# Two folded cross attentions in a twelve-block network: query folding in pieces among the steps, normalisation in two halves, the output projection in two parts, the last batch in halves

## The chip, the cores and the metric

The kernel runs on one core of one Trainium2 chip. It is one program that computes a whole Perceiver-like network of twelve blocks in float32. The metric is the device time of one execution in microseconds (us), taken from the first to the last instruction, as a median over runs. The engines are TensorE (PE in the profile, with PEld for its weight loads), VectorE (DVE), ScalarE (ACT), GpSimd (POOL) and SyncE (SP, here a DMA queue).

## The reference

Twelve blocks follow each other, each with a residual connection. The change touches the two blocks marked below; they are the same computation with different weights, on a batch of 16, with 64 queries of width 256 and a context of 1024 keys of width 192 for each element.

```python
def _layernorm(x, axis=-1, eps=1e-05):
    m = jnp.mean(x, axis=axis, keepdims=True)
    v = jnp.var(x, axis=axis, keepdims=True)
    return (x - m) / jnp.sqrt(v + eps)

def _L1_xattn_ref(x, context, Wq, Wk, Wv, Wo, bo):      # _L2_xattn_ref computes the same
    h, d = (8, 64)
    scale = d ** (-0.5)
    q = (x @ Wq).reshape(B, Sq, h, d).transpose(0, 2, 1, 3)
    k = (context @ Wk).reshape(B, -1, h, d).transpose(0, 2, 1, 3)
    v = (context @ Wv).reshape(B, -1, h, d).transpose(0, 2, 1, 3)
    scores = jnp.einsum('bhid,bhjd->bhij', q, k) * scale
    attn = jax.nn.softmax(scores, axis=-1)
    out = jnp.einsum('bhij,bhjd->bhid', attn, v)
    out = out.transpose(0, 2, 1, 3).reshape(B, Sq, h * d)
    return out @ Wo + bo

x = x + _L0_xattn_ref(...)   # then _L0_attn_ref, _L0_ffn_ref
x = x + _L1_xattn_ref(_layernorm(x, axis=-1), ctx_768, ...)   # touched by the change
...                          # _L1_attn_ref, _L1_ffn_ref
x = x + _L2_xattn_ref(_layernorm(x, axis=-1), ctx_768, ...)   # touched by the change
...                          # _L2_attn_ref, _L2_ffn_ref, and the three blocks of L3
```

## The kernel before

The 1024 tokens (16 batch elements of 64 queries) lie in `X` as eight tiles of 128 tokens; `xn` is the normalised form and `xnT` its transpose. `xattn_folded` computes both touched blocks, called with `"L1_xattn"` and `"L2_xattn"`; below they are the second and the third cross attention. Keys are never projected: the query is multiplied by the key weights instead ("folded"), so that scores are `qw` times the raw context.

- **Prologue.** `norm_T` (lines 244 to 262) normalises and transposes all eight tiles, in two halves of four tiles. After it every instruction of TensorE, VectorE and ScalarE is put into a fixed order by `set_order(True)`: each engine's instructions are chained in the order of the Python text (`in_order`, line 172). What is issued through plain `nc.…` calls, POOL work and DMAs, is placed by the framework's scheduler.
- **Folding.** `queries(g, m)` projects two heads (index `m`, four of them) for a group `g` of four batch elements into a bank `psq`, which ScalarE scales into `qT`. `fold(g, m)` multiplies by the key weights into two banks `psqw`, one copied into `qw` by VectorE, one by ScalarE. `folded(g)` does all four `m` in a row: once in the prologue, and then in front of the first scores of every next group, three times. `qw` has one buffer for a whole group.
- **Steps.** There are 32 steps, one for each batch element `b` and half `h` of the eight heads. In step `i` TensorE computes the scores of the step ahead (four banks `pss`; first the 128 rows of context, then `sums` of the present step into `psm`, then the other 64 rows), and then the `values` of the batch element before (four of eight key chunks a step), and in odd steps its `others` (the remaining 64 context channels). VectorE takes the reciprocal of the sums, the row minimum of the negated scores (`least`: tiles `nm`, `nw`, `nmm`), half of the `shares` (normalising the probabilities), and two 32-by-32 transposes (`turn`, tile `pT`). ScalarE does the other half of the shares, the eight `exps` (tile `pr`), and copies.
- **Output.** `keep` copies the finished sums into `oc`. After every four batch elements, in the even step of the next but one, `output(g2)` projects by the value weights (`pso`, copied to `oT`) and by the output weights (`psy`), and adds into `X`.
- **PSUM banks.** `ps_s` has five banks in turn (tag `s`: `pss`, `psq`, `psqw`, one `pso`); `ps_t` has one (tag `t`: `psm`, one `pso`, `psy`); `ps_o` has two (`o0`, `o1`).
- **Extra work in the steps.** In the second cross attention `conv_taps` (POOL, ScalarE and VectorE, tile `tapp`) runs in steps 3 to 11 for the block after. In the third `ctx_sigma` runs on VectorE in every odd step (eight pairs of statistics, then a root on POOL). `add_row` adds the output's bias to all eight tiles of `X` on POOL (eight instructions, line 157); it is ordered behind the last root.

The order inside a step is the order of this text:

```python
prs, sm = now
if ahead:
    pss = scores(*ahead, lambda: sums(st, sm))
dve.reciprocal(sm, st["sum"][:, :8])
shares(prs, sm, 1)
if ahead:
    now = exps(pss, least(pss))
shares(prs, sm, 0)
turn(b, 2 * h, prs[0])
```

Of the kernel before, what the change touches and what calls it, by code (L numbers as in the profile page):

```python
# [15 lines left out]
P = 128  # L16
# [62 lines left out]
class Net:  # L79
# [428 lines left out]
    def xattn_folded(self, L):  # L508
# [18 lines left out]
        with ExitStack() as es:  # L527
# [9 lines left out]
            self.norm_T(ps_s, "s")  # L537
            self.set_order(True)
            qws, qTs, ctxs, cxs, pTs, outs, ocs = ({} for _ in range(7))

            def bank(name):
                return ps_s.tile([P, 512], F32, tag="s", name=name)

            def queries(g, m):
# [3 lines left out]
                ps = bank("psq")  # L548
# [4 lines left out]
            def fold(g, m):  # L553


                if m == 0:
                    qws[g] = two.tile([P, 2, G, H, TQ], F32, tag="qw", name="qw", bufs=1)
                qT = qTs[m]
                pss = [bank("psqw") for _ in range(2)]
# [4 lines left out]
                for hh, copy in enumerate((dve.tensor_copy, act.copy)):  # L564
                    copy(qws[g][:, :, :, 2 * m + hh, :], pss[hh].rearrange("p (i b q) -> p i b q", i=2, q=TQ))

            def folded(g):
                queries(g, 0)
                for m in range(4):
                    if m < 3:  # L570
                        queries(g, m + 1)
                    fold(g, m)
# [17 lines left out]
            def scores(b, h, between):  # L590
# [4 lines left out]
                qw = qws[b // G]  # L595
                pss = [bank("pss") for _ in range(4)]

                def score(k, u, i, rows, start, stop):
                    for qa in range(4):
                        self.mm(  # L600
                            pss[k][qa * 32 : (qa + 1) * 32, u * 256 : (u + 1) * 256],
                            qw[rows, i, b % G, 4 * h + k, u * 32 : (u + 1) * 32],
# [66 lines left out]
            def values(b, r):  # L669

                if r == 0:
                    outs[b] = [ps_o.tile([P, 512], F32, tag=n, name=n) for n in ("o0", "o1")]
                for j in range(4 * r, 4 * r + 4):
                    self.mm(outs[b][0], cxs[b][:, j, 0:P], pTs[b][:, j], j == 0, j == NKC - 1)

            def others(b):

                for j in range(NKC):
                    rows = slice((j % 2) * 64, (j % 2 + 1) * 64)
                    self.mm(outs[b][1][rows, :], cxs[b][:, j, P:C], pTs[b][:, j], j < 2, j >= NKC - 2)  # L680
# [8 lines left out]
            def output(g2):  # L689
                oc = ocs[g2]  # L690
                oT = one.tile([P, 4, T2], F32, tag="oT", name="oT")
# [14 lines left out]
                for tt in range(T2 // P):  # L706
                    t = g2 * T2 // P + tt
                    ps = ps_t.tile([P, 512], F32, tag="t", name="psy")
                    for m in range(4):
                        self.mm(ps[:, :D], oT[:, m, tt * P : (tt + 1) * P], wo[:, m, :], m == 0, m == 3)  # L710
# [44 lines left out]
            for r in range(2):  # L755
                values(B - 1, r)
# [1921 lines left out]
```

## Time and profile before

| what | value |
|---|---|
| runs | 3168.56, 3169.97 and 3195.57 us; median 3169.97 us |
| profiled execution | 3170.8 us, of which the span of its instructions is 3168.8 us |
| TensorE busy | 2940.9 us, 93% of the span |
| VectorE, ScalarE, GpSimd busy | 1960.3, 1348.4, 712.7 us |
| mean granted TensorE clock | 0.953 |
| second cross attention, first scores to last `psy` matmul | 766.8 to 1207.5 us |
| third cross attention, first scores to last `psy` matmul | 1659.2 to 2098.6 us |

A busy TensorE is not one that works at its peak: the ends of matmuls are modelled, and a matmul at half the granted clock counts as busy for twice as long. The stage tables give the granted clock beside the busy times. In a timeline, a bracket behind an instruction says how long its engine had stood idle and what released it.

### The profile page before, as it was taken

How to read it: one execution, taken by the hardware profiler on the slowest of the kernel's cores; microseconds unless marked ns; L12 is line 12 of the kernel's file. 1: busy time of each engine (PE TensorE's matmuls, PEld its weight loads, DVE VectorE, ACT ScalarE, POOL GpSimd, SP SyncE). 2: the span in 40 equal slices, each digit the busy share in tenths (PEclk: the TensorE clock that was granted, in tenths of full speed). 3: DMA queues.
4: the chain of work that ended last, by engine and by line, in shares of the span. 5: the costliest groups of instructions: out<-in, count | busy, mean ns of one | idle time of the engine just before them, and what ended most of it. 6: DMA issues, size and time to landing. Idle time of an engine off the chain costs nothing.

```text
span 3168.8 us, 64106 instructions
## 1 busy us (share of the span) xinstructions
PE 2940.9 (93%) x26912; PEld 1772.9 (56%) x26912; DVE 1960.3 (62%) x4061; ACT 1348.4 (43%) x3035; POOL 712.7 (22%) x784
## 2 busy tenths in 40 slices
PE   7999999898899999979978999997999899998797
PEld 4666666665445544458854545434665455556676
DVE  6888886524666665971127676757884676765611
ACT  3555554312554541013324454438861255654211
POOL 1000002411110001014411000024771355541131
PEclk9999999999999999978988999998999999999889
DMA  2000000013223313017851222201111211210233
GB/s 74 32 32 32 28 22 15 14 37 105 61 78 92 98 45 82 21 65 270 294 162 53 70 71 73 59 21 39 41 54 37 64 57 63 70 44 14 94 108 122
DMA packets 73793, 223.00 MB, mean 70 GB/s; under 512 B 17457, under 2 KB 28580, under 8 KB 66594
## 3 DMA queue, kind: packets, MB, share of 16 engines
q1 hardware_dynamic: 45936, 113.99, 11.9%
q0 software_dynamic: 21840, 99.39, 9.4%
q10 hardware_dynamic: 5730, 5.53, 0.6%
q8 instruction: 212, 3.47, 0.5%
q14 instruction: 75, 0.61, 0.1%
HBM read 210.00 MB, written 12.66 MB: 70 GB/s over the span
## 4 chain that ended last, share of the span: by engine, by line
PE 79%; DVE 9%; issue 4%; ACT 4%; POOL 3%; DMA 1%; SPq 0%; ACTq 0%; POOLq 0%; DVEq 0%
PE pss L188 13%; PE o L188 12%; PE pu L188 6%; PE psp L188 5%; PE pkv L188 5%; PE pd L188 5%; PE py L188 4%; PE pst L191 4%; PE psc L188 3%; PE po L188 2%; DVE nm L72 2%; ACT pr L72 2%; PE pb L191 2%; PE psi L188 1%; PE psq L188 1%
## 5 line engine op out<-in xcount | busy, mean ns | idle before, releaser
L188 PE MATMUL pss<-cT,qw 128*32 128x256 f32 x8192 | 371.5, 387 | 23.0 <-ACT pr L72 23.0
L72 DVE TENSOR_REDUCE nm<-pss 128x2 f32<-128x512 f32 (+1 forms) x384 | 309.3, 861 | 86.3 <-PE pss L188 86.3
L188 PE MATMUL o<-pT,cx 128*64 128x512 f32 (+1 forms) x1024 | 355.4, 607 | 0.0
L72 ACT ACTIVATE pr<-pss,nmm 128x256 f32<-128x256 f32 x512 | 234.3, 483 | 164.8 <-DVE nmm L72 164.8
L188 PEld LDWEIGHTS pss<-cT,qw 128*32 128x32 f32 x8192 | 205.0, 110 | 173.0 <-ACT pr L72 33.1
L188 PEld LDWEIGHTS o<-pT,cx 128*64 128x64 f32 (+1 forms) x1024 | 127.8, 165 | 200.2 <-issue 187.8
L205 POOL TENSOR_SCALAR rs<-mv 128x8 f32<-128x8 f32 (+3 forms) x52 | 10.0, 193 | 877.1 <-DVE mv L221 444.4
L188 PE MATMUL pkv<-wx,cT 128*128 128x512 f32 (+1 forms) x512 | 193.3, 632 | 0.6 <-issue 0.6
L72 ACT ACTIVATE pr<-pr,sm 128x256 f32<-128x256 f32 x256 | 109.1, 497 | 184.2 <-DVE sm L72 184.2
L72 DVE TENSOR_SCALAR pr<-pr,sm 128x256 f32<-128x256 f32 (+1 forms) x384 | 170.6, 486 | 6.6
L72 DVE TENSOR_TENSOR_SCAN h<-dA,pb 128x512 f32<-128x512 f32 x128 | 154.5, 1217 | 15.8 <-PE pb L191 9.4
L1444 POOL TENSOR_TENSOR h<-h,cb 128x1024 f32<-128x1024 f32 x64 | 151.4, 2368 | 53.3 <-DVE h L72 51.0
L2304 DVE TENSOR_SCALAR y<-pd,row 128x256 f32<-128x256 f32 x39 | 18.9, 484 | 225.1 <-PE pd L188 175.7
L72 DVE STREAM_TRANSPOSE pT<-pr 128x1024 f32<-128x1024 f32 x128 | 151.8, 1224 | 2.2
L188 PE MATMUL pd<-wd,hT 128*128 128x256 f32 x656 | 149.3, 382 | 3.0 <-DVE hT L2492 1.4
L72 ACT ACTIVATE pr<-pss,nm 128x1024 f32<-128x1024 f32 x128 | 142.5, 1113 | 11.4 <-DVE nm L72 8.8
L191 PE MATMUL pst<-ident,pr 128*128 128x128 f32 x1024 | 140.6, 280 | 5.8 <-DVE sm L72 1.9
L72 ACT COPY pT<-pst 128x512 f32<-128x512 f32 x128 | 74.9, 585 | 163.8 <-PE pst L191 163.8
L191 PEld LDWEIGHTS pst<-ident,pr 128*128 128x128 f32 x1024 | 109.4, 141 | 61.5 <-ACT pT L72 26.5
L188 PEld LDWEIGHTS pd<-wd,hT 128*128 128x128 f32 x656 | 123.1, 190 | 31.4 <-DVE hT L2492 6.2
L1618 POOL TENSOR_TENSOR rnk<-rnk,mhalf 128x8 f32<-128x8 f32 (+1 forms) x84 | 130.0, 1548 | 7.0
L188 PE MATMUL py<-h,ident 128*128 128x512 f32 x256 | 130.7, 596 | 0.0
(525 smaller groups left out, 5700.2 us busy)
## 6 DMA issues: line engine op xcount, KB each, us to landing
cT<-in_ctxT SPq DMA_DIRECT2D x32, 768.0 KB, 4.4
cx<-in_ctxP SPq DMA_DIRECT2D x32, 768.0 KB, 4.3
cT<-in_ctxT SPq DMA_DIRECT2D x32, 512.0 KB, 4.3
cT<-in_ctxT SPq DMA_DIRECT2D x64, 256.0 KB, 6.1
offb<-d_off SPq DMA_DIRECT2D x16, 576.0 KB, 3.6
cb<-d_C SPq DMA_DIRECT2D x16, 512.0 KB, 3.8
wu<-in_L_ffn_w POOLq DMA_DIRECT2D x8, 1024.0 KB
wd<-in_L_ffn_w POOLq DMA_DIRECT2D x8, 1024.0 KB
```

What stands on the lines that cost most here:

```text
L72: ins = getattr(self.engine, op)(*args, **kwargs)
L188: self.in_order(self.nc.tensor.matmul(out, lhsT=lhsT, rhs=rhs, start=start, stop=stop))
L191: self.in_order(self.nc.tensor.transpose(out, in_, self.ident))
L205: nc.gpsimd.tensor_scalar(t[:p, :n], in_, scale, eps, ALU.mult, ALU.add)
L1444: nc.gpsimd.tensor_tensor(hs[i], hs[i], cbs[hf, g], ALU.mult)
L1618: nc.gpsimd.tensor_tensor(r, r, self.mhalf[:, : n * H], ALU.pow)
L2304: nc.vector.tensor_scalar(y[:, i, :], po[:, i * D : (i + 1) * D], weight[:, g + i : g + i + 1], None, ALU.mult)
```

## The change

`norm_T` in the prologue gives way to `norm(g)` and `normed(g)` for four tiles each: `norm(0)` and `normed(0)` stay in the prologue, `norm(1)` comes at the end of step 1 and `normed(1)` at the end of step 2. `folded` is gone. `queries` and `fold` are called for one piece (two heads of a group) at a time: pieces 0 and 1 of group 0 ahead of the first scores, pieces 2 and 3 behind the first `exps`; the pieces of group 1 in steps 0, 1, 6 and 7, of group 2 in steps 10, 12, 14 and 15, of group 3 in steps 18, 20, 22 and 23. `qw` becomes three buffers of half a group's heads. `psq` and one of the two `psqw` move from the five banks to the single bank of `ps_t`. `output` is cut into `heads` (in the even step, as before) and `output(t)` for two tiles at the end of the odd step behind it. In the last step the `values` of the element before go ahead of the `sums`, and the last batch element's `values` and `others` are computed for 256 of 512 columns at a time. `add_row` moves from step 2 to step 5.

```diff
-            self.norm_T(ps_s, "s")
...
+            def norm(g):
+                ts = slice(4 * g, 4 * g + 4)
+                for t in range(4 * g, 4 * g + 4):
+                    dve.bn_stats(stats[:, t, :], self.X[:, t, :])
+                    dve.bn_aggr(mv[:, t, :], stats[:, t, :])
+                self.rsqrt(rs[:, ts], mv[:, ts, 1], 1.0, 1e-5, 4)
+            def normed(g):
+                for t in range(4 * g, 4 * g + 4):
+                    dve.tensor_scalar(
+                        self.xn[:, t, :], self.X[:, t, :], mv[:, t, 0:1], rs[:, t : t + 1], ALU.subtract, ALU.mult
+                    )
+                for c, copy in enumerate((dve.tensor_copy, act.copy)):
+                    ps = bank("psT")
+                    for k in range(4):
+                        self.tr(ps[:, k * P : (k + 1) * P], self.xn[:, 4 * g + k, c * P : (c + 1) * P])
+                    copy(self.xnT[:, c, g * 512 : (g + 1) * 512], ps)
 
             def queries(g, m):
-                ps = bank("psq")
+                ps = ps_t.tile([P, 512], F32, tag="t", name="psq")
...
             def fold(g, m):
-                if m == 0:
-                    qws[g] = two.tile([P, 2, G, H, TQ], F32, tag="qw", name="qw", bufs=1)
+                if m % 2 == 0:
+                    qws[g, m // 2] = two.tile([P, 2, G, 4, TQ], F32, tag="qw", name="qw", bufs=3)
                 qT = qTs[m]
-                pss = [bank("psqw") for _ in range(2)]
+                pss = [bank("psqw"), ps_t.tile([P, 512], F32, tag="t", name="psqw")]
...
-            def values(b, r):
+            def values(b, js, cols=slice(0, 512)):
...
-            def output(g2):
+            def heads(g2):
...
+            def output(t):
+                ps = ps_t.tile([P, 512], F32, tag="t", name="psy")
...
-            folded(0)
+            norm(0)
+            normed(0)
+            for m in range(2):
+                queries(0, m)
+                fold(0, m)
             steps = [(b, h) for b in range(B) for h in range(2)]
             pss = scores(0, 0, None)
             now = exps(pss, least(pss))
+            for m in range(2, 4):
+                queries(0, m)
+                fold(0, m)
+            pieces = {8 * g + at: (g + 1, m) for g in range(B // G - 1) for m, at in enumerate((2, 4, 6, 7))}
+            pieces.update({0: (1, 0), 1: (1, 1)})
+            del pieces[2], pieces[4]
             for i, (b, h) in enumerate(steps):
                 ahead = steps[i + 1] if i + 1 < len(steps) else None
-                if ahead and ahead[0] % G == 0 and ahead[1] == 0:
-                    folded(ahead[0] // G)
+                piece = pieces.get(i)
...
                 else:
+                    values(b - 1, range(4, NKC))
                     sums(st, sm)
                 dve.reciprocal(sm, st["sum"][:, :8])
                 shares(prs, sm, 1)
+                if piece:
+                    queries(*piece)
                 if ahead:
                     now = exps(pss, least(pss))
                 shares(prs, sm, 0)
                 turn(b, 2 * h, prs[0])
                 turn(b, 2 * h + 1, prs[1])
-                if b > 0:
-                    values(b - 1, h)
-                    if h == 1:
-                        others(b - 1)
-                        keep(b - 1)
+                if ahead and b > 0:
+                    values(b - 1, range(4 * h, 4 * h + 4))
+                if piece:
+                    fold(*piece)
+                if b > 0 and h == 1:
+                    others(b - 1)
+                    keep(b - 1)
+                if i == 1:
+                    norm(1)
+                if i == 2:
+                    normed(1)
                 if h == 1 and L == "L2_xattn":
                     self.ctx_sigma(b, cxs[b], dve)
-                if b == 1 and h == 0:
+                if i == 5:
                     self.add_row(f"{L}_bo", one)
-                if h == 0 and b % G2 == 1 and b > 1:
-                    output(b // G2 - 1)
+                if b % G2 == 1 and b > 1:
+                    if h == 0:
+                        heads(b // G2 - 1)
+                    else:
+                        for tt in range(T2 // P):
+                            output((b // G2 - 1) * T2 // P + tt)
...
-            for r in range(2):
-                values(B - 1, r)
-            others(B - 1)
+            for cols in (slice(0, 256), slice(256, 512)):
+                values(B - 1, range(NKC), cols)
+                others(B - 1, cols)
             keep(B - 1)
-            output(B // G2 - 1)
+            heads(B // G2 - 1)
+            for t in range(NT - T2 // P, NT):
+                output(t)
```

More of the change, by code (lines that the diff above doesn't have):

```diff
@@ L564, in fold @@
                 for hh, copy in enumerate((dve.tensor_copy, act.copy)):
[L565 to L572, printed above, removed]
+                    copy(
+                        qws[g, m // 2][:, :, :, 2 * (m % 2) + hh, :], pss[hh].rearrange("p (i b q) -> p i b q", i=2, q=TQ)
+                    )
             def load(b):
```

33 lines of the change are left out of this document (18 added, 15 removed).

## The prediction

> **What bounds the kernel now.** I read the page's busy times and chain first, then TensorE's timeline through both blocks, then stage tables with the granted clock.
>
> ```profile
> PE 2940.9 (93%) x26912; PEld 1772.9 (56%) x26912; DVE 1960.3 (62%) x4061; ACT 1348.4 (43%) x3035; POOL 712.7 (22%) x784
> PE 79%; DVE 9%; issue 4%; ACT 4%; POOL 3%; DMA 1%; SPq 0%; ACTq 0%; POOLq 0%; DVEq 0%
> ```
>
> TensorE is the bound. Here an edit gains only where it removes or fills one of TensorE's waits; moved matmuls are paid again where they land. TensorE's timeline of the second cross attention shows the waits in brackets:
>
> ```profile
> 766.81 6.55 PE L188 MATMUL pss<-cT,qw 128*32 128x256 f32 x144
> 777.64 4.48 PE L188 MATMUL pss<-cT,qw 128*32 128x256 f32 x48 [4.28 <-ACT pr L72]
> 788.05 4.48 PE L188 MATMUL pss<-cT,qw 128*32 128x256 f32 x48 [3.00 <-ACT pr L72]
> ...
> 859.81 2.08 PE L188 MATMUL psqw<-qT,wkT 64*128 64x256 f32 x8 [4.57 <-ACT qT L72]
> ...
> 916.40 1.99 PE L188 MATMUL psy<-wo,oT 128*128 128x256 f32 x8 [1.31 <-DVE oT L72]
> 918.91 1.99 PE L188 MATMUL psy<-wo,oT 128*128 128x256 f32 x8 [0.51 <-DVE X L72]
> ...
> 968.04 1.13 PE L188 MATMUL psqw<-qT,wkT 64*128 64x256 f32 x8 [1.64 <-ACT qT L72]
> ```
>
> They are the first steps (no values to fill them), each `folded` (its `qT` stands behind eight exps on ScalarE), each `output`, and the last step:
>
> ```profile
> 1178.15 0.30 PE L188 MATMUL psm<-sm,same 128*32 128x8 f32 x8 [3.10 <-ACT pr L72]
> 1178.38 20.79 PE L188 MATMUL o<-pT,cx 128*128 128x512 f32 x56
> 1199.00 0.60 PE L188 MATMUL pso<-oc,wv 128*64 128x256 f32 x4
> ```
>
> Steps between them are gapless: `pss` starts at 880.38, 889.53 and 902.27, so 9.15 us and 12.74. A wait costs twice where the clock falls behind it; the stage table (span, PE, PEld, DVE, ACT, POOL, clock, DMA) after the 4.28 us wait reads 0.58:
>
> ```profile
> 778.00:782.00 4.00, 4.00 (x56) 2.07 (x46) 0.00 (x0) 2.31 (x11) 0.00 (x0) 0.58 0.01 4
> ```
>
> 48 scores matmuls take 4.48 us there against some 2.6 at full clock, about 1.8 more; I use 1.7 a wait.
>
> **Rows I add up.** A piece's `psq` and `psqw` 1.03 us each (pitch 1.06 from 863.60 on); `qT` 0.38; a `qw` copy 0.69 on VectorE, 0.585 on ScalarE; hand-overs 0.06 to 0.2. Scores 5.5 (808.40 to 813.92). From scores' start to their first exp 8.5 in the steady state (808.40 to 816.92), 9.75 at first (766.81 to 776.56, with a table load); eight exps 3.76.
>
> **Second cross attention, part by part.**
>
> *Prologue.* The first half of `xnT` is copied by 752.3; `psq` then waits no more for the second half (755.57, 757.71). Two pieces in a row: 4 x 1.03, two waits for `qT` of 0.64, one of 0.85 because `psqw` and the next `psq` share `ps_t` and ScalarE must first empty it: 6.25. Scores start at 758.6, 8.2 us early. But pieces 2 and 3 come behind the exps in ScalarE's order: 758.6 + 9.75 + 3.76 = 772.1. Then 0.5 (`qT`), 2.06 (`psqw` at half clock, TensorE having idled 7 us), 0.85, 1.7, 0.64, 1.03, so the next scores start at 778.9 and their exps at 787.4, against 786.98 before. Gain: -0.4 (+1.3 if the clock holds, -2 if it stays low). The whole early start is given back.
>
> *Steps 0 and 1.* The exps-to-exps loop was 10.41 (786.98 to 797.39). `psq` and `psqw` land in its 3.0 us wait and keep the clock up: about 9.5. Gain 1.8. VectorE's `qw` copy and `norm(1)` (4 x 0.55) fit its own 3.0 us of idle (2.28 + 0.70 before the reciprocal and `nm`); without that cover they would cost their 2.9.
>
> *Step 2.* `normed(1)` puts eight transposes into TensorE's queue ahead of scores(2,0), and they wait for VectorE: exps at 787.4 + 19.0 = 806.4, turns done 3.45 later (816.86 to 820.3), then four `xn` (1.38 in the rows) and transposes and hand-overs of 1.6, until 812.9. Before, those scores started at 808.40. Behind the wait queue the scores, and behind these the exps. That is 4.5 late after 1.4 gained: it costs 5.9 (bounds 0, if the turns came early enough, and 8, if `norm(1)` is late too).
>
> *`add_row`.* It ran at 758 to 764, under the folding. Now it can first run behind the root of `norm(1)`, into steps 2 and 3. The third cross attention shows what that costs VectorE:
>
> ```profile
> 1700.11 5.54 POOL L157 TENSOR_TENSOR X<-X,row 128x256 f32<-128x256 f32 x8
> 1700.52 0.34 DVE L72 COPY nw<-nm 64x8 f32<-64x8 f32 x1
> 1700.89 0.64 DVE L72 TENSOR_TENSOR nw<-nw,nm 64x8 f32<-64x8 f32 x1
> ```
>
> Six small ones, 0.15 to 0.18 each elsewhere, take 0.34 to 0.67: 2.5 us on the way to the exps. Cost 2.5 (0 if it falls in slack, 5.5 if the taps' POOL work queues behind it).
>
> *Folding.* The first `folded` spans 852.08 to 867.65, 15.57 us, because the taps delay its `qT`. Two pieces remain, 4.1, in steps 6 and 7, and `psq` waits for `ps_t` until the reciprocal has read `psm`; the taps make that late (837.29 for a `psm` of 833.76), 1.85 and 1.23: gain 8.4. The other two span 9.71 each (964.51 to 974.22); four pieces cost 8.24 each: gain 2.9, less 1.85 for step 10, still among the taps: 1.1. The `qw` copies hide in VectorE's idle and behind the exps.
>
> *Output.* Gone: 1.31, 0.51, 0.52, 0.51. New: in steps 10 and 18 `pso` needs `ps_t`, which ScalarE empties (`qw`) only behind its exps: scores end 0.75 after the first `nm`, then 1.03 + 3.5 + 1.03 to 6.3, exps run to 7.5, the copy to 8.1: about 1.7, and 2.4 plus 0.4 of clock among the taps. The second `psy` still waits 0.5 for `X`. Loss 3.2.
>
> *Last step.* From 1175.05 to `pso` 23.95 us. New: values 3.5, `psm` 0.15, others 3.7, 0.9 for `keep` to free `o0`, then two halves of 3.5 + 1.85: 18.9, all at full clock. Twice the weight loads hide under matmuls (0.19 against 0.21, half the pitch of 512 columns). Gain 5.1.
>
> Sum: -0.4 + 1.8 - 5.9 - 2.5 + 8.4 + 1.1 - 3.2 + 5.1 = **4.4 us gained**.
>
> **Third cross attention.** *Prologue*: `xnT`'s half is ready at 1647.4 either way, and TensorE is at half clock after 19.78 us of idle: 6.25 + 2.06 gives 1655.8; + 13.5 + 6.8 + 8.5 = 1684.6 for the second exps, against 1680.40: loss 4.2. *Steps 0 to 2*: before, 31.4 from there to the end of scores(2,0) (1711.82), with the `add_row` collision in it. Now 9.5, then 9.5 + 3.6 (`norm(1)` and `ctx_sigma`, 6.6 with the copy, overrun VectorE's 3.0 idle), 3.45 turns, 3.0 transposes, 5.5 scores, so 34.6; a little more for the slow clock: loss 3.5. *Folding*: 9.71 + 11.35 + 9.72 against ten pieces of 2.06 in full steps: gain 10.2. *Output*: three waits of 0.52 go; `pso` waits 1.7 twice, and the second `psy` 2.1 three times, because its bank's `X` add now queues behind `ctx_sigma` on VectorE (sigma ends 2039.88, `psy` would be done at 2038.2): loss 8.1. *`add_row`* in step 5, with slack: loss 0.8 (0 to 2.5). *Last step*: 2067.37 to 2090.11 was 22.74: gain 3.9. Sum: **2.5 us lost**.
>
> DMA: no load binds. The first context's last piece lands at 759.1 and is needed after 762; loads keep their steps.
>
> Together 1.9 us gained: 3170.8 - 1.9 = 3168.9 by the profiled execution, which lies 0.8 above the median of the runs; so **3168**.
>
> **A rule that speaks on the new waits.** After a wait of 2.46 us (1705.43) the clock read 0.63, and after one of 1.65 (1858.72) it read 0.70, though four other waits of 1.64 or 1.65 left it at 1.00. The Trainium skill, "TensorE: Matmul & The Clock Gate", section "Why this matters for your kernels", lets gaps up to about 3 us pass without harm; by that rule alone the sum would be 3168 with no chance of more from this side. For the value I take no loss of clock, since four of five rows at that length show none; for the range 1.7 for each of ten new waits (`pso` four, `psy` three, `psq` three), which is 3185.
>
> **Rivals.**
> 1. *The early start is kept*: 8.2 and 2 us at the prologues, no wait at step 2 (5.9 + 3.5), no output waits (11.3), no `add_row` cost (3.3), the third's start not cold (4.2): 38.4 in all, 3168 - 38 = 3130. For it: 8 us of idle TensorE lie between the first scores and exps. Against: ScalarE's fixed order. A faster result by 1% needs nearly all of this.
> 2. *Half of that*: step 2 and outputs wait less than reckoned, 3150.
> 3. *The one bank `ps_t` becomes the bound* (slower): each piece in a full step, 20 in all, waits for VectorE's reciprocal before `psq`, and the next user for ScalarE's copy after `psqw`. If the 1.85 and 1.7 us of the worst steps held for every piece, 20 x 3.55 = 71, less the 4.9 of `psq` waits counted above, makes 3234. It decides where VectorE runs over 2 us late at the reciprocal; before, it did so in the taps' steps alone, so in few of the 20.
> 4. *Clock drops* behind ten waits: 3185.
> 5. *It doesn't do what it says*: pieces in gapless steps hide nothing, they are only moved; gains and costs cancel: 3171.
>
> **How the numbers follow.** Forecast 0.5 (with rival 5, 3160 to 3176), rival 2 0.19, rival 1 0.06, rival 4 0.2, rival 3 0.05. The range of 8 in 10 leaves out rivals 1 and 3: 3148 to 3187. About 1% (32 us) is what a measurement of this kernel can tell from no change: faster 0.08 (rival 1 and the end of 2), within 0.86, slower 0.06.
>
> **What would show it.** Right: first scores of the second cross attention some 8 us earlier but its second exps at the same distance from the block's start; a `psT` wait of 4 us (second) and 7 us (third) in step 2; `pso` waiting for ScalarE, `psy` 2 us for VectorE in the third; no `psm` wait of 3.1; the block's length from the last `pd` to `pso` 4 to 5 us less, in the third 2 to 3 more. Wrong: `psq` waits in most pieces, or none of the new waits.

## The result, and the profile after

The changed kernel takes 3205.95 us (median of 12 runs, 3199.25 to 3213.32) where the kernel before, measured beside it, took 3177.27 (12 runs, 3168.56 to 3199.78). The ratio on record is 1.0078, with a 95% interval of 1.0053 to 1.0104: slower by 0.8%. (The two medians alone would give 1.0090.) The prediction was 3168 with a range up to 3187. The profiled execution took 3205.8 us with a span of 3204.1 us and a mean granted clock of 0.943; the one before had 3168.8 and 0.953. So the two profiles differ by 35 us where the medians differ by 28.7: the profiled execution of the kernel before is one of its shorter ones.

The two lines of the page that the prediction began with now read:

```profile
PE 2969.2 (93%) x26976; PEld 1796.2 (56%) x26976; DVE 1960.2 (61%) x4061; ACT 1347.6 (42%) x3035; POOL 712.1 (22%) x780
PE 77%; DVE 10%; issue 5%; ACT 4%; POOL 3%; DMA 1%; SPq 0%; POOLq 0%; ACTq 0%; DVEq 0%
```

TensorE is busy 28 us longer, though the change adds only 64 instructions to it. Where the clock is not 1.00 in these profiles it is 0.50, so a mean of 0.953 says that TensorE stood at half clock for 2 x 0.047 x 3168.8 = 298 us, and 0.943 says 365. That is 67 us more at half clock, worth up to 34 us of work.

The next table says where. I divided TensorE's timeline by blocks and subtracted (us; in brackets, the time at half clock, from the clock records). A cross attention counts from the end of the last matmul before it, so that its first wait belongs to it; the other blocks count from their first matmul that isn't a transpose, and the last row ends with the last matmul:

| block | before | after | difference |
|---|---|---|---|
| up to the second cross attention | 748.7 (17) | 746.8 (17) | -1.9 |
| second cross attention | 461.8 (31) | 462.4 (24) | +0.6 |
| convolution (`mamba_conv`), not touched | 188.6 (20) | 206.0 (59) | **+17.4** |
| its feed-forward, not touched | 225.7 (41) | 226.7 (47) | +1.0 |
| third cross attention | 475.6 (48) | 484.8 (58) | **+9.2** |
| scan (`mamba1`), not touched | 292.5 (48) | 296.3 (53) | +3.8 |
| its feed-forward, not touched | 98.9 (0) | 104.7 (12) | +5.8 |
| the rest | 660.5 (82) | 660.3 (82) | -0.2 |

So 28 of the 35 us were lost in blocks that the diff does not touch. The largest is the last stage of the convolution, where a projection of 512 columns (`psi`) alternates with 32 tiny matmuls of 8 columns (`psT`). TensorE's timeline there, first of the kernel before, then of the changed one (start, duration, group):

```profile
1359.32 1.13 PE L188 MATMUL psi<-xnT,w_in 128*128 128x512 f32 x2
1360.38 1.10 PE L188 MATMUL psT<-xt,T 64*64 64x8 f32 x32
1361.41 1.88 PE L188 MATMUL psi<-xnT,w_in 128*128 128x512 f32 x2
1363.22 1.88 PE L188 MATMUL psT<-xt,T 64*64 64x8 f32 x32
```

```profile
1337.10 1.13 PE L188 MATMUL psi<-xnT,w_in 128*128 128x512 f32 x2
1338.16 1.10 PE L188 MATMUL psT<-xt,T 64*64 64x8 f32 x32
1339.19 2.02 PE L188 MATMUL psi<-xnT,w_in 128*128 128x512 f32 x2
1341.14 1.88 PE L188 MATMUL psT<-xt,T 64*64 64x8 f32 x32
```

Nothing waits in either: no bracket stands behind a line. The same matmuls take nearly double the time from one moment on, and this moment comes 26.4 us after the stage's start in the kernel before (1335.03 to 1361.41) and 5.5 us after it in the changed one (1333.68 to 1339.19). The stage tables show what happens there (columns: stretch, length, busy time of PE, PEld, DVE, ACT, POOL, then clock, DMA share, GB/s); before, then after:

```profile
1350.00:1360.00 10.00, 10.00 (x171) 6.48 (x170) 10.00 (x15) 1.75 (x3) 0.00 (x0) 1.00 0.01 2
1360.00:1370.00 10.00, 10.00 (x104) 5.89 (x102) 10.00 (x24) 1.75 (x3) 0.00 (x0) 0.58 0.01 2
```

```profile
1340.00:1350.00 10.00, 10.00 (x94) 5.80 (x92) 10.00 (x12) 1.06 (x2) 0.00 (x0) 0.50 0.01 2
```

In 1360 to 1370 and in 1340 to 1350 TensorE is recorded as 100% busy, and its clock is halved all the same.

In the second cross attention the lines that answer to those shown before are:

```profile
752.27 2.20 PE L191 MATMUL psT<-ident,xn 128*128 128x128 f32 x8 [5.48 <-DVE xn L72]
761.09 5.55 PE L188 MATMUL pss<-cT,qw 128*32 128x256 f32 x128
774.92 2.08 PE L188 MATMUL psqw<-qT,wkT 64*128 64x256 f32 x8 [7.22 <-ACT qT L72]
782.33 5.61 PE L188 MATMUL pss<-cT,qw 128*32 128x256 f32 x64
793.80 3.81 PE L188 MATMUL pss<-cT,qw 128*32 128x256 f32 x64 [1.22 <-ACT pr L72]
...
817.32 0.80 PE L191 MATMUL psT<-ident,xn 128*128 128x128 f32 x2 [4.46 <-DVE xn L72]
820.36 5.37 PE L188 MATMUL pss<-cT,qw 128*32 128x256 f32 x64
...
863.16 1.13 PE L188 MATMUL psq<-xnT,wq 128*128 128x256 f32 x4 [0.89 <-DVE sm L72]
...
920.34 3.67 PE L188 MATMUL pso<-oc,wv 128*64 128x256 f32 x32 [2.16 <-ACT qw L72]
```

The predicted waits are all there: `qT` behind the exps (7.22), the transposes of step 2 (4.46), `psq` behind the reciprocal (0.89), `pso` behind ScalarE (2.16). What the prediction had too small is the price behind them: 64 scores matmuls take 5.61 us at 782.33 and 5.37 at 820.36, against 3.66 at full clock.

### The profile page after: what moved, and what is told of

It is laid out like the page before. It is cut to its first block, busy times and chain, and to the rows that moved or that the text cites. A ratio compares the mean times of both kernels' runs of the same rounds, so it can differ in the third digit from the quotient of the medians.

```text
span 3204.1 us, 64211 instructions
## 1 busy us (share of the span) xinstructions
PE 2969.2 (93%) x26976; PEld 1796.2 (56%) x26976; DVE 1960.2 (61%) x4061; ACT 1347.6 (42%) x3035; POOL 712.1 (22%) x780
## 4 chain that ended last, share of the span: by engine, by line
PE 77%; DVE 10%; issue 5%; ACT 4%; POOL 3%; DMA 1%; SPq 0%; POOLq 0%; ACTq 0%; DVEq 0%
PE pss L188 13%; PE o L188 11%; PE psp L188 5%; PE pu L188 5%; PE pkv L188 5%; PE pd L188 5%; PE py L188 4%; PE pst L191 4%; PE psc L188 3%; DVE nm L72 2%; PE po L188 2%; ACT pr L72 2%; PE psi L188 2%; PE pb L191 2%; PE psq L188 1%
## 5 line engine op out<-in xcount | busy, mean ns | idle before, releaser
L188 PE MATMUL o<-pT,cx 128*64 128x512 f32 (+3 forms) x1088 | 349.7, 574 | 2.0 <-PE o L188 2.0
L188 PEld LDWEIGHTS o<-pT,cx 128*64 128x64 f32 (+1 forms) x1088 | 135.9, 163 | 182.8 <-issue 169.1
```

The lines of the kernel that those rows point to most:

```text
L188: self.in_order(self.nc.tensor.matmul(out, lhsT=lhsT, rhs=rhs, start=start, stop=stop))
```

## The experiments

Distances below are taken from the block's start, so that a block's own time can be read apart from what happened earlier. Each run's own time and trace are used. The kernel before was timed again with each set of runs: 3171.55 (19 runs, 3165.83 to 3193.93) beside the first four, 3190.23 (19 runs, 3168.34 to 3197.00) beside the next four, 3169.94 (13 runs, 3166.28 to 3181.29) beside the last four. By itself it moves by 30 us, and mostly between two groups, about 3166 to 3182 and 3188 to 3200. The middle set (`e5` to `e8`) ran on another chip than the other two, so times are compared within a set wherever that is possible; block lengths come from one profiled execution of each kernel.

### Only the place in time is changed

`e3_after_delay` adds work to the changed kernel:

```
             ...
+            ps = mid.tile([P, 512], F32, tag="m", name="psw")
+            for n in (512, 512, 192):
+                self.mm(ps[:, :n], w_in[:, 0, :P], self.xnT[:, 0, :n])
             for g in range(2):
                 tokens(g)
```

> The changed kernel with three useless matmuls (about 2.05 us of TensorE) just ahead of the convolution's last stage, which keeps its order. Theory A: only the place of the stage in the 3.41 us windows changes. By the place that the profile after shows, a delay of 2.05 us puts the first window under 40% at the sixth or seventh instead of the second: the stage takes 37 to 46 us instead of 56, and the kernel gets faster by 8 to 19 us although work is added: 3187 to 3198. Runs may scatter by some 20 us, because a shift of 0.2 us decides which window is the first. Theory B: the added work is paid: 3208 us, the stage as long as in the profile after.

Measured: 3181.8 us (10 runs: eight from 3172.3 to 3185.3, two at 3203.5 and 3205.9), 1.0035 of the kernel before (1.0005 to 1.0064). Useless work made the kernel about 24 us faster (3205.95 to 3181.8, but these are medians of two sets of runs; between the two profiles it is 20.7). The convolution block took 186.5 us instead of 206.0, which is 19.5 of it. The second cross attention stayed as it was (463.3); the third took 480.4 instead of 484.8, although nothing was changed in it. The halving now comes late:

```profile
1366.02 1.12 PE L188 MATMUL psi<-xnT,w_in 128*128 128x512 f32 x2
1367.07 1.10 PE L188 MATMUL psT<-xt,T 64*64 64x8 f32 x32
1368.11 1.76 PE L188 MATMUL psi<-xnT,w_in 128*128 128x512 f32 x2
1369.79 1.88 PE L188 MATMUL psT<-xt,T 64*64 64x8 f32 x32
```

`e10_before_delay` does the reverse to the kernel before:

```
+            ps = mid.tile([P, 512], F32, tag="m", name="psw")
+            for n in (512, 512):
+                self.mm(ps[:, :n], w_in[:, 0, :P], self.xnT[:, 0, :n])
```

> The kernel before, with two useless matmuls (about 1.75 us) ahead of the convolution's last stage, nothing else. Theory A: the same lottery of 3.41 us windows that cost the changed kernel 17 us is lost here on purpose. By the place that the profile before shows, the first window under 40% comes some 8 us after the stage's start instead of 27, the clock halves there, and the stage takes about 57 us instead of 41: the block 188.6 + 1.8 + 15 = 205 us, the time 3185 to 3198. Rival (the stage of the kernel before is robust, only the change disturbs it): the block 190 us, 3172 us.

Measured: 3184.69 us (10 runs, eight of them from 3183.1 to 3187.7, two at 3165.7 and 3166.6) where all 13 runs of the kernel before beside it stayed at or below 3181.3; ratio 1.0029 (1.0009 to 1.0049). The block took 205.2 us, the 205 expected, and the clock halves 7 us after the stage's start at 1335.10:

```profile
1341.10 1.10 PE L188 MATMUL psT<-xt,T 64*64 64x8 f32 x32
1342.13 1.78 PE L188 MATMUL psi<-xnT,w_in 128*128 128x512 f32 x2
1343.84 1.88 PE L188 MATMUL psT<-xt,T 64*64 64x8 f32 x32
```

The mean granted clock, on record for every run, tells the same of the runs that were not profiled. In `e10` the two short ones have 0.955, the eight long ones 0.947 to 0.949; in `e3` the two long ones have 0.944 and 0.945, the eight short ones 0.950 to 0.956. It also parts the two groups of the kernel before: in the middle set five runs of 3168.34 to 3181.08 us have 0.949 to 0.953, and fourteen of 3188.2 to 3197.0 have 0.943 to 0.946.

So the 17 us of the convolution were lost because the stage begins at another place in time, and this place belongs to a train of windows. The lengths of all half-clock stretches are multiples of 3.41 us (3.4, 6.8, 10.2, 13.7 and so on; a last one that the end of the profile cuts off is left out), and their edges stand on one grid in each profile. I took, for the five profiled kernels whose stage kept its order, the share of each such window in which a `psi` is recorded. All five halvings came right after a window of 0.44. Two windows of 0.44 passed without one, and none of the 17 windows with 0.46 or more was followed by one. By these shares the stage stands close to a limit, and a shift by a fraction of 3.41 us can decide. The share alone doesn't settle it, as the two windows without a halving show. The Trainium skill, "TensorE: Matmul & The Clock Gate", section "What's actually happening", describes a window of 3413 ns that runs freely and does not start with the kernel; the multiples of 3.41 us agree. The page speaks of idle and busy windows; that a window without any recorded idle time can halve the clock is what these profiles add.

### Taking the lottery away: one failure, one cure

The first idea was a finer alternation. `e1_before_fine` and `e2_after_fine`:

```
-                    self.mm(ps, w_in[:, k, c * P : (c + 1) * P], self.xnT[:, k, cols], k == 0, k == 1)
+                W = 512 if c < 4 else 256
+                for at in range(0, 512, W):
+                    ...
+                        self.mm(ps[:, at : at + W], w_in[:, k, c * P : (c + 1) * P], x, k == 0, k == 1)
...
-                    if d % (TB // 4) == 0:
+                    if d % (TB // 8) == 0:
```

> The kernel before, with one thing changed in the convolution block behind the second cross attention: its 16 input projections of 512 columns, which alternate with 32 tiny matmuls each (64x8, the local convolution), are cut into 32 of 256 columns and alternate with 16. Theory A (clock windows): the granted clock is decided in windows of 3.41 us; a window in which the wide matmuls fill under about 40% is followed by half clock for the rest of the stage. In the profile before the share falls to that in the eighth window (drop at 1361.7 us), in the profile after in the second (1339.3). In the finer order no window has less than about 46%, so the stage runs at full clock: some 34 us from the first tiny matmul to the last against 39 us before, and the kernel takes 3164 us where the profiled run before took 3171, with a smaller spread between runs than the 31 us seen. Theory B (the stage is slow for another reason, a transfer or a memory conflict): 3171 to 3178, the stage as long as before.

Measured: 3194.2 us (3192.5 to 3196.5), 1.0071 of the kernel before (1.0047 to 1.0095): slower. The block took 207.6 us.

> The changed kernel with the same finer order in the convolution block. Theory A: that stage takes 34 us instead of 56, so the kernel takes about 3183 us instead of 3206, and what is left against the same edit of the kernel before (about 19 us) is what the two attentions themselves and other clock drops cost. Theory B (the change makes this stage itself slower, by its data or its buffers): 3200 us or more, the stage still over 50 us.

Measured: 3201.68 us (3197.3 to 3203.7), 1.0094 (1.0068 to 1.0119); block 210.5. The expectation failed in both. The pitch of the groups offers a reason:

```profile
1341.58 0.70 PE L188 MATMUL psi<-xnT,w_in 128*128 128x256 f32 x2
1342.21 0.64 PE L188 MATMUL psT<-xt,T 64*64 64x8 f32 x16
1342.78 0.70 PE L188 MATMUL psi<-xnT,w_in 128*128 128x256 f32 x2
1343.41 0.64 PE L188 MATMUL psT<-xt,T 64*64 64x8 f32 x16
```

A pair takes 1.20 us (1341.58 to 1342.78) and holds half a projection. A whole projection streams for 0.87 us by the dense `psc` rows (13.90 us for 32 records, two to a projection), so the share is 0.43 of 1.20 us, 36%, where the coarse order has 0.87 of 2.09, 42%. The reading is that halving the projections added weight loads and lowered the mean below the limit, so that no place in the train is lucky. It fits that both kernels lost, and so does a limit at about 0.4 of streaming time, between the two orders; no run here separates the share from the mere number of small groups.

The cure is to give the tiny matmuls denser company. `e5_before_fill`, `e6_after_fill`:

```
-            for c in range(1, 4):
-                for n in range(2):
-                    conv(c, n)
-                ...
+            for c, n in ((1, 0), (1, 1), (3, 0), (3, 1), (2, 0)):
+                conv(c, n)
+                ...
+            sums.append(taps(2, 0, HB))
             for g in range(2):
                 tokens(g)
-            for i in range(P // TB):
-                toeplitz(i, (n for h in range(2) for n in project(4 + i, h)))
+            rest = convs(2, 1)
+            for i in range(2):
+                toeplitz(i, rest)
+            sums.append(taps(2, HB, B))
+            rest = (n for c in range(4, 8) for h in range(2) for n in project(c, h))
+            for i in range(2, 4):
+                toeplitz(i, (n for j, n in enumerate(rest) if j % 2))
```

> The kernel before with the convolution block reordered so that its tiny matmuls always stand beside dense work: channel 3 is convolved before channel 2, the second half of channel 2's convolution (16 matmuls of 0.87 us) goes between the tiny matmuls of the first half of the stage, two to every 16, and the 16 input projections between those of the second half, two to every 16; VectorE takes channel 2 in two halves. The same matmuls, in another order. Theory A, mended after the finer order (which dropped in every run): what counts is the share of a 3.41 us window in which columns stream. The old order has 0.87 of 2.09 us (42%), the finer order, with its extra weight loads, 0.43 of 1.19 (36%), so it fell earlier; the new order has 1.74 of 2.9 (60%). Expected: no half clock between 1320 and 1370 us, the block (first projection to the router) at 185 to 190 us against 188.6 in the profile before, and no runs 25 us above the others: 3165 to 3172. Rival (alternating itself lets the clock fall, whatever the share): the block at 205 us or more, 3190.

Measured: 3176.64 us (10 runs, 3171.9 to 3181.8), 0.9968 of the kernel before (0.9947 to 0.9989), which in these runs mostly sat in its upper group. It is above the 3165 to 3172 expected. The scatter fell from 29 us to 10, and the clock holds through the stage:

```profile
1340.00:1350.00 10.00, 10.00 (x142) 6.16 (x141) 10.00 (x28) 2.44 (x4) 0.75 (x1) 1.00 0.28 86
1350.00:1360.00 10.00, 10.00 (x111) 5.66 (x112) 9.97 (x29) 2.44 (x4) 0.00 (x0) 1.00 0.01 2
1360.00:1370.00 10.00, 8.76 (x114) 5.24 (x112) 10.00 (x21) 2.43 (x4) 0.70 (x1) 1.00 0.17 35
1370.00:1380.00 10.00, 0.00 (x0) 0.00 (x0) 9.97 (x36) 0.00 (x0) 0.00 (x0) 0.51 0.05 19
```

The block took 192.0 us, more than the 185 to 190 expected: the last row shows TensorE with nothing to do while VectorE is at 9.97 of 10. VectorE's taps, whose operations for channel 2 take 62 us in two halves where they took 49 in one, now end the block.

> The changed kernel with the same reordered convolution block. Theory A: the block takes 185 to 190 us instead of 206, so the kernel takes about 3186 us instead of 3206; against the same edit of the kernel before it is 12 to 18 us slower (0.6 in the second cross attention, 5 to 9 in the third, 4 to 8 of half clock in the blocks behind it). Rival (the change makes this block slower by itself): 3200 or more.

Measured: 3194.5 us (10 runs, 3184.1 to 3199.6), 1.0016 of the kernel before (0.9993 to 1.0038); block 192.1 instead of 206.0. The rival falls by the block's length: the change does not slow this block by itself. The time is 8.5 above the 3186 expected. Between the two filled kernels 18 us remain in the medians (3194.5 less 3176.6), the upper end of what was expected. The profiled execution of e6 was its fastest, so 8 us are seen in the traces (spans 3182.4 and 3174.7) and the other 10 are not; the granted clock of its other runs, 0.948 to 0.953 against 0.952 in the profiled one, says that most of them spent longer at half clock, but not in which block.

The small losses in the two later blocks are of the same kind. `e5` has the attentions of the kernel before, and yet its scan takes 296.7 us and its feed-forward 104.4, like the changed kernel's (296.3 and 104.7). The first 12 us of that feed-forward, in the kernel before and then in `e5`:

```profile
2393.00:2405.00 12.00, 12.00 (x53) 7.20 (x52) 6.14 (x16) 4.43 (x5) 2.06 (x3) 1.00 0.08 23
```

```profile
2393.00:2405.00 12.00, 12.00 (x41) 9.17 (x40) 2.91 (x12) 3.41 (x4) 1.50 (x2) 0.52 0.08 23
```

Clock 1.00 against 0.52, with the same program there. And `e2`, which has the change, takes 98.9. The third cross attention scatters in the same way without any change to it: 475.6 us in the kernel before and 476.0 in `e1`, but 471.2 in `e5` and in `e10`, with 10 us less at half clock.

### The start of the attentions

`e4_fine_prologue` puts the start back in the changed kernel with the finer convolution (which costs its 20 us there); `e7_prologue_fill` does the same with the filled one:

```
-            norm(0)
-            normed(0)
-            for m in range(2):
-                queries(0, m)
-                fold(0, m)
+            self.norm_T(ps_s, "s")
+            ...
+            queries(0, 0)
+            for m in range(4):
+                if m < 3:
+                    queries(0, m + 1)
+                fold(0, m)
...
-            for m in range(2, 4):
-                queries(0, m)
-                fold(0, m)
...
-                if i == 1:
-                    norm(1)
-                if i == 2:
-                    normed(1)
```

(In both, `psq` and `psqw` of the first folding take banks of `ps_s` again.)

> The changed kernel with the finer convolution, and with the start of both cross attentions put back: all eight tiles normed and transposed first, all four pieces of the first folding ahead of the first scores; add_row stays in step 5, the other pieces, the outputs and the last batch stay as changed. Theory P (prologue and step 2 lose more than predicted): against the finer changed kernel the first projection of outputs comes 9 to 11 us earlier in the second cross attention and 10 to 13 us earlier in the third, together some 20 us: about 3163. Rival (only the wait for the transposes in step 2 counts, as the prediction sized it: 5.9 + 3.5, and 4.6 at the prologues): 14 us, 3169. Rival (the clock decides, not the order): within 5 us of the finer changed kernel.

Measured: 3169.02 us (10 runs, 3160.3 to 3173.9), 0.9978 (0.9956 to 0.9999), with a convolution of 210.4 us. Second cross attention 448.5 us, third 464.5: 14.0 and 16.1 less than with the same convolution and the changed start (462.5 and 480.6). The 30 us together are more than the 20 expected and more than the rival's 14; the time still lies above the 3163 expected.

> The changed kernel with the reordered convolution block, and the start of both cross attentions as before (all tiles normed first, four pieces ahead of the first scores). By the finer pair of runs the second cross attention then takes 448 to 449 us and the third 464 to 465, against 461.8 and 475.6 before: 14 and 16 less than the changed kernel, 3153 to 3158 in all, faster than the kernel before by some 0.5%. Rival (those block lengths came from clock windows that fell well in that one run): 3165 or more.

Measured: **3149.15 us** (3147.1 to 3154.6), 0.9883 of the kernel before (0.9843 to 0.9923), whose runs there sat high; against the lowest of the three medians of the kernel before (3169.94, on the other chip) it is 0.9934, and the three relatives of e7 below, on that chip, have 0.9924 to 0.9945. Attentions 446.5 and 466.7.

`e8_whole_norm` separates the two parts of the start:

```
             norm(0)
+            norm(1)
             normed(0)
+            normed(1)
...
-                if i == 1:
-                    norm(1)
-                if i == 2:
-                    normed(1)
```

> The changed kernel with one thing put back: all eight tiles are normed and transposed at the start; the last two pieces of the first folding still come behind the first exps. If the order of the pieces costs the most: the second cross attention stays within 5 us of the changed kernel's 462.4. If the transposes that wait in step 2 (predicted 5.9 and 3.5) with their half clock cost the most: it gets 8 to 12 us shorter, 450 to 454, and the third likewise.

Measured in one run only, of 3180.64 us: 458.9 and 474.8 us. In the second cross attention that is only 3.5 less than the changed kernel, so there the order of the pieces costs the most; in the third it is 5.6 to 10 less (changed kernels: 480.4 to 484.8). Distances from the block's start, in us, show both parts apart:

| second cross attention | before | after | e8 | e4 |
|---|---|---|---|---|
| first scores | 18.1 | 14.3 | 19.2 | 18.1 |
| first `psm` | 33.2 | 41.0 | 45.1 | 33.2 |
| first values | 56.1 | 62.4 | 66.5 | 56.1 |
| first `pso` | 162.7 | 173.6 | 168.4 | 158.0 |
| last `pso` | 450.3 | 450.9 | 447.4 | 437.0 |

From the first scores to the first `psm`: 15.1 us with four pieces ahead, 26 to 27 with two pieces behind the exps. From the first values to the first `pso`: 101.9 with the whole norm at the start (e8, e4), 111.2 with the norm by four tiles. The order loses 10.8 to 11.6, the split 9.3, and the split gives back 4 to 5 by starting earlier. The 9.3 doesn't rest on one profile each: `e2` and `e6` have 111.2 as well, `e3` 109.9, and `e7` and `e9` 101.9. The lines of e8 and of e4:

```profile
766.22 5.55 PE L188 MATMUL pss<-cT,qw 128*32 128x256 f32 x128
771.70 1.13 PE L188 MATMUL psq<-xnT,wq 128*128 128x256 f32 x4
780.05 2.08 PE L188 MATMUL psqw<-qT,wkT 64*128 64x256 f32 x8 [7.23 <-ACT qT L72]
```

```profile
767.75 6.55 PE L188 MATMUL pss<-cT,qw 128*32 128x256 f32 x144
778.57 4.48 PE L188 MATMUL pss<-cT,qw 128*32 128x256 f32 x48 [4.28 <-ACT pr L72]
```

With the pieces behind the exps, TensorE waits 7.23 us for `qT`, longer than the 4.28 for the banks, and then has the pieces still to do, at half clock (2.08 for a `psqw` of 1.13).

### The outputs, and two attempts at a better start

`e9_outputs_back` (from e7):

```
-                if b % G2 == 1 and b > 1:
-                    if h == 0:
-                        heads(b // G2 - 1)
-                    else:
-                        for tt in range(T2 // P):
-                            ...
+                if h == 0 and b % G2 == 1 and b > 1:
+                    heads(b // G2 - 1)
+                    for tt in range(T2 // P):
+                        ...
```

> The version with the old start and the reordered convolution (3149 us), with the outputs' projection put back into one step: heads and both tiles pairs of output in the even step, as before. The prediction's loss here (3.2 in the second cross attention, 8.1 in the third) would make this version faster by some 5 to 11 us. Against it: with the projection in one step its four output matmul groups again wait for oT (1.31 us in the profile before) and X (0.51) and nothing in that step hides it; the trace of the changed kernel shows pso waiting 2.15 and 1.59 us and psy 0.51 either way. Expected by the trace: the second cross attention within 2 us of 446.5, the third within 3 of 466.7, the time within 4 us of 3149.

Measured: 3148.13 us (3144.8 to 3151.7), 0.9924 (0.9904 to 0.9943), no different from e7's 3149.15 (which is from the other chip). From the first `pso` to the last, the second cross attention takes 279.0 us against e7's 278.9, the third 277.4 against 283.8 (and 281.7 in e4). So by these profiles the split of the outputs costs nothing in the second and 4 to 6 us in the third, which the whole time doesn't show. There the second `psy` waits for VectorE's addition behind `ctx_sigma` (in e7 1.98, 2.35 and 1.98 us, in e9 0.58, 0.51 and 0.51). The line of the changed kernel:

```profile
1853.32 2.48 PE L188 MATMUL psy<-wo,oT 128*128 128x256 f32 x8 [1.97 <-DVE X L72]
```

`e11_early` (from e7) and `e12_early_split` (from e11):

```
-            for m in range(4):
-                if m < 3:
+            for m in range(2):
+                if m < 1:
...
-            now = exps(pss, least(pss))
+            queries(0, 2)
+            m = least(pss)
+            fold(0, 2)
+            queries(0, 3)
+            fold(0, 3)
+            now = exps(pss, m)
```

```
-            self.norm_T(ps_s, "s")
+            norm(0)
+            normed(0)
+            turned(0)
...
+                if i == 1:
+                    norm(1)
+                if i == 2:
+                    normed(1)
+                if i == 3:
+                    turned(1)
```

> The version with the old start and the reordered convolution (3149 us), with the early start kept in a form that ScalarE's order allows: pieces 0 and 1, then the first scores, then pieces 2 and 3, and only then the first exps (VectorE takes the maxima between). TensorE's idle time before the second scores (4.28 us, and the half clock behind it) is filled by the two pieces, and the first scores start 4 us earlier; the exps come up to 3 us later behind their scores. Expected: each cross attention 2 to 5 us shorter, 3140 to 3146. Rival (the one bank that pieces 2 and 3 share makes them 6.6 us long, and the exps wait for all of it): no gain or 2 us slower.

> The same, and the norm by four tiles again, but with the second four's transposes one step behind their normalisation (in step 3, VectorE's part in step 2), so that TensorE doesn't wait for VectorE. If the wait in step 2 was what made the norm by four tiles lose (3.5 us in the second cross attention and 6 to 10 in the third), the split now gains: the first scores start some 3 us earlier in the second cross attention (5 in the profiles without the split) while the eight transposes cost 2.2 in step 3: 0 to 3 us shorter each, 3136 to 3145. Rival (VectorE's 2.2 + 1.4 us in steps 1 and 2 delay the exps whatever the order): 3 to 6 us slower than without the split.

Measured: 3150.37 us (3146.8 to 3155.1), 0.9939 (0.9917 to 0.9961), and 3152.06 (3147.7 to 3157.5), 0.9945 (0.9924 to 0.9966). Neither differs from e7, and both miss what was expected (3140 to 3146, and 3136 to 3145). The room for the pieces is seen on ScalarE in the changed kernel, which stood idle for 7.72 us ahead of its first exps:

```profile
769.55 1.28 ACT L72 ACT_TABLE_LOAD   x1 [7.72 <-DVE nmm L72]
```

In e11 two pieces fill it, and the long wait is gone from TensorE's timeline:

```profile
770.20 1.13 PE L188 MATMUL psqw<-qT,wkT 64*128 64x256 f32 x8 [0.53 <-ACT qT L72]
772.11 1.07 PE L188 MATMUL pss<-cT,qw 128*32 128x256 f32 x16 [0.78 <-DVE qw L72]
774.37 2.90 PE L188 MATMUL pss<-cT,qw 128*32 128x256 f32 x48 [1.18 <-ACT pr L72]
```

First `psm` 31.4 us from the start against 32.6 in e7, and 48.3 against 49.8 in the third: a gain of 1.2 and 1.5, less than the 2 to 5 expected, and in the third it is given back later. The split with late transposes gains 3.5 more at the third's start (44.8) and loses 3.1 between the first values and the first `pso` (104.5 against 101.4). The start is worth little once it no longer loses.

## Why the prediction was wrong, point by point

**The step that failed is the frame of the sum.** The prediction added up the two attentions and let every block behind them stand at its old length. Its statement on what follows them was about loads ("no load binds"), and it treated the clock as a price on a few waits inside the blocks (rival 4). The block table puts 28 of the 35 us into blocks that follow an attention and that the diff doesn't touch. e3 and e10 show that the convolution's part comes from where its stage stands in the 3.41 us windows, since a delay alone takes it away or brings it about; e5 shows the same loss in the last feed-forward and in the scan without the change. No rival had such a mechanism, and the row that could have warned was in the profile before: 0.58 at 1360 to 1370, in a stretch without a single wait.

**The start of the second cross attention** was put at -0.4 and steps 0 and 1 at +1.8; together, by the distance of the first values from the block's start, they measured -6.3 (56.1 against 62.4). The mechanism was right (pieces behind the exps, the early start given back), the term was too small. From the block's start, the second exps were predicted at 38.7 us (787.4) and came at 45.9 (792.73), 7.2 later. The first scores, predicted at 9.9, came at 14.3. The prediction took the first half of `xnT` to be ready when it was before; but the first four tiles' transposes started 5.5 us into the block instead of 1.3, because they waited for VectorE (5.48), and the first `psq` ran at half clock (1.71). Then the clock, reckoned slow for 2.06 us, stayed at half from 772.7 to 786.3, so that a `psq`, both `psqw` and most of the scores of 5.61 us were all slow. The gain of steps 0 and 1 was as predicted (1.5 by the loss of 7.8 at the first `psm` and of 6.3 at the first values, where 1.8 was put).

**Step 2.** Predicted -5.9 by a wait of about 4.5; the wait was 4.46, the cost by e8 and e4 9.3 (111.2 against 101.9). What was missed is again the clock behind it (5.37 us for scores of 3.66) and four `xn` of 2.16 us in place of 1.38; how the 9.3 divides was not measured. `add_row` did run beside VectorE in this step, as predicted: one small operation takes 0.64.

**Folding, outputs, last batch.** By e4, which has these and the old start, the second cross attention gains 13.3 us (461.8 to 448.5); the prediction had 8.4 + 1.1 - 2.5 - 3.2 + 5.1 = 8.9. The last step was right: 27.64 us from the last scores to `pso` before (1171.36 to 1199.00), 22.84 after (1174.82 to 1197.66), with the second half of the earlier batch's values now ahead of `psm`; the gain is 4.8, in the third 3.6 (predicted 5.1 and 3.9). `psq` waited 0.89, 0.74 and 0.89 where 1.85, 1.23 and 1.85 were put, and `pso` 2.16 and 1.59 where 2.8 and 1.7 were put. e9 shows that the split of the outputs cost nothing here.

**The third cross attention** was put at -2.5 and measured -9.2 in the profile after, -4.8 to -5.7 in e2, e3 and e6, against the 475.6 of the kernel before; against the 471.2 that the same code takes in e5 and e10 it would be 4.4 more. Its start (first values 73.4 to 80.2, -6.8) and its step 2 (111.0 against e8's 101.4, -9.6) are the mis-sized terms, predicted together at -7.7 (the wait itself in step 2, 7.04 us, was as forecast); the split of the outputs, put at -8.1, cost 4 to 6.

**The rivals.** Rivals 1, 2 and 5 (3130, 3150, 3171) did not happen; the 3149 of e7, near rival 2's figure, has another start and another convolution and doesn't bear it out. Rival 3 did not happen: `psq` waits for `ps_t` at the start (0.71 us) and in three steps of the taps (0.74 to 0.89), not in every piece; the outputs' waits are 0.51 to 2.16. Rival 4 named the right mechanism, the clock, but put it behind waits; in the convolution, where half of the 35 us came, nothing waits.

**Still open.** Where exactly the limit lies (0.44 of recorded time halved the clock five times out of seven), why the kernel before falls into two groups more in some sets of runs than in others, in which block most runs of e6 lose the 10 us by which they exceed its profiled one, and how much of the difference between the sets belongs to the chip.

## What to carry to other kernels

Look up, ahead of any sum, the stretches in which the granted clock is below 1.00 without a wait: here such a stage sat at a limit, and an edit upstream that moved it by about 2 us cost or gave 15 to 20. Give such stages denser work, and compare edits by the length of the touched block as well as by the whole time. An early start is worth only what the in-order queue behind it lets through: work that the next step needs goes ahead of the exps, not behind them.

## What the runs showed of the hardware that was not expected

The clock halved in stretches in which TensorE was recorded 100% busy, with only 36 to 42% of the time streaming columns by the estimate above; with 60% (1.74 of 2.9 us, by the same estimate) it held. At half clock 32 matmuls of 8 columns took 1.88 us instead of 1.10, and a projection of 1.12 took 2.07. The place of the windows relative to the kernel's first matmul was not the same in each set of profiles, but near within two of the sets: 2.86 and 2.89 us into the 3.41 in the first pair, 1.69 to 2.07 in the last four, scattered over 1.24 and 1.6 us in the others. That would let most runs of one set win or lose the same lottery, and may be why the kernel before had a median of 3170 in one set and 3190 in another; the other chip of that set is a rival, and neither was tested.
